# An output product in two slots and its sum in the third, weight sums at other places, a folded product loaded in place, and a gate behind a mask

## The chip, the cores and the metric

The kernel runs on one core of a Trainium2 chip, as one launch. The metric is the device time of that launch in microseconds. All arithmetic is in float32. Each float32 matrix product appears in the profile as two matmul records, and what the text calls one product is those two records.

## The reference

The input x is 8 sequences of 128 rows of 512 numbers. Two layers are computed, each of the form x = x + ffn(cond(x)).

- First layer. cond multiplies each sequence by one of 8 matrices of 512x512, chosen by an index. ffn is a 512x512 product with a bias, plus 8 experts of rank 16 of which the two with the largest gate values count, with softmax weights.
- Second layer, cond. Attention with 32 query heads and 8 key heads of 128 numbers: queries, keys and values are projected from x, queries and keys are normalised by their root mean square and rotated by their position, keys and values of 512 earlier positions come from 16 pages of a cache, positions beyond the sequence's length are masked, and after the softmax the outputs of all heads are multiplied by Wo (4096x512).
- Second layer, ffn. 64 experts of rank 8, of which the 16 with the largest scores count: `gate` is the softmax over the 16 largest of (x Wq_w^T) keys^T, and the output is ((x A_w^T) * gate) B_w^T * 2.

```python
probs = jax.nn.softmax(scores, axis=-1)
o = jnp.einsum('bhqk,bkhd->bqhd', probs, v_all)
...
gate = jnp.sum(jax.nn.one_hot(top_idx, NUM_EXPERTS, dtype=top_w.dtype) * top_w[..., None], axis=-2)
z_gated = (z * gate[..., None]).reshape(*z.shape[:-2], BOTTLENECK)
out = jnp.einsum('bsn,on->bso', z_gated, B_w) * SCALING
```

## The kernel before

**Units.** The attention is cut into 64 units, one for each of the 8 sequences and each of the 8 key heads, in the order: two key heads of a sequence, then the next sequence; after 16 units the next two key heads. A unit has four query heads, h = 0 to 3. `iteration(u)` writes the instructions of unit u, and with them, in the same four slots, work of other units: the output product of unit u-3, projections of units to come, and sums. The order of the instructions on each engine is written out by hand: what the program says first, an engine does first, and waits come only from the data. u runs from 1 to 66 (`NU` = 64). In the text r is u modulo 16.

**A slot (unit u, head h)** has: the two score products on TensorE (`scores`, L445 against the cached keys, L448 against the unit's own), into one of two PSUM buffers in turn; the mask and the row minimum on VectorE in one instruction (`mask_exp`, L458: the scores come negated, so "low" is what the exponential is shifted by); the exponential with its row sum on ScalarE (L469); for the head before it the reciprocal on VectorE (L474) and the multiplication on POOL (`normalize`, L475); from h = 2 on the transpose by 32x32 blocks on VectorE (`blocks`, L480, for head h-2). In slot 2 the queries of the unit after next are transposed as well (`blocks_qk`, L431), into the same buffer `pb`, of which there is one: it is free when the last unit's transfer out has read it. Then the output product and a part of the projections on TensorE (`project`, L268, with adds on VectorE, L271).

**The end of a unit**: `add_output(u-3, False)`, the copy of the next unit's queries and keys on ScalarE (`heads_qk`, L1019), weight loads on POOL's queue, `normalize` of head 3, `norms(u+3)` (squares on ScalarE, L317; then on POOL ss, L321, and rs, L323), `blocks` of heads 2 and 3, `exchange_out` (px, four DMAs, two on SP's and two on ScalarE's queue), `add_output(u-3, True)`, `rotate(u+3)` on VectorE (two L335 of 128x512, two L349, which need rs, then L352 and L353), and `values(u-2)` on TensorE (L1032). At the start of the next unit SP's queue holds page loads of keys, the query part of what was sent out (qkb), more page loads and the probabilities (pT), each behind the transfer out.

**The output product.** Four units (a pair of sequences, two key heads) and the parts of Wo for these two key heads, in two halves, are multiplied in the manner of Strassen and Winograd, with seven block products (`output`, L1157). v = u-3 is split into a pair p and a turn t = v modulo 4; turn 1 is u = 4, 8, 12, ..., 60. Up to p = 13 (u = 56) turn 1 has one product, A11 times B11, in four parts, one for each slot:

```python
elif t == 1 and p < WHOLE_PAIRS:
    product(0, (p, A11), B11, (h,))
```

Its result lies in the one PSUM buffer "y", which all turns use. `add_output(v, late)` adds it to the four quarters of the pair's output (`over(lo, 4)`: L1244 copies it for the first four pairs, L1226 adds it afterwards, 128x1024) as a late add, after `exchange_out`. Turn 2's first product writes the same buffer.

**Weight sums.** The projections use seven products as well, whose right sides are four parts of the weights (0 to 3, loaded by `load_q` at places listed in `LOADS_Q`) and four sums, T3, T2, T4 and T1 in the order in which they depend on each other (`sums_q`, L163, 128x768). Each group of 16 units needs new ones for two key heads: `sums_w` says in which slot and on which engine. Product 6 in slot 3 of r = 11 (and of r = 13 for the second key head) needs T2, product 7 at that unit's end needs T3, product 4 in slot 1 of the next unit needs T4, product 5 in its slot 2 needs T1.

**The ffn of the second layer** begins in the last units. Wq_w and keys are multiplied ahead (`l0_fold`) and kept in DRAM as `fold_d`, 128 x 4 x 64. `f_weights`, from unit 57 on, loads it and A_w and B_w into a tile `fw`; its part "sa" has, for each of four chunks, 64 columns "s" (the folded product) and 512 columns "a" (A_w). `fold_d` is first loaded into a part of its own, "f", and copied to "s" on VectorE (`f_fold`, L856) in slot 1 of unit 59. At the end of unit 59 `f_first_products(0)` multiplies the first sequence's rows (fq and fr, L987), copies two halves away on ScalarE, adds the scores and at once makes the gate's weights (`f_weights_of`, L891 to L908: two times the eight largest, an exponential on ScalarE, sum and reciprocal). Before fq, slot 2 of unit 59 has the transposes of those rows and their copy on ScalarE (L866).

## Time and profile before

| | |
|---|---|
| median of 3 runs | 1203.69 us (1202.99 to 1205.12) |
| the profiled execution | 1204.42 us, span 1202.7 us |
| TensorE | 1187.0 us busy (99%) |
| VectorE | 937.2 us (78%) |
| POOL (GpSimd) | 773.3 us (64%) |
| ScalarE | 507.1 us (42%) |
| L1157, the output products | 206.6 us busy, 784 records |
| L163, weight sums on POOL | 26 of 1.82 us |
| L163, weight sums on VectorE | 6, of 0.93 to 2.56 us |
| L856, the copy of the folded product | 1 of 2.82 us |

The profile is of one execution; PE is TensorE's matmuls, PEld its weight loads, DVE is VectorE, ACT ScalarE, POOL GpSimd, SP SyncE, which here issues transfers. A line of a timeline has the start and the length in microseconds, the engine, the line of the kernel, the operation, the tiles written and read, the shape and the count, and in brackets how long the engine had been idle and what ended that. A line of the waits has who waited for whom, the sum in microseconds, how often, and the longest. Ends of matmuls are modelled; the distance from one start to the next is measured.

### The profile page before, as it was taken

The numbers are of one execution on the slowest core, as the hardware profiler recorded it, in microseconds if no ns is written. First come the engines' busy times: TensorE is split into PE (matmuls) and PEld (weight loads), VectorE is DVE, ScalarE is ACT, GpSimd is POOL, SyncE is SP. The second block draws the span as 40 slices with busy tenths as digits, with TensorE's granted clock in tenths as the row PEclk, the third lists the DMA queues.
The fourth block names the chain that finished last, engine by engine and source line by source line (L and its number), as shares of the span: only waits on it lengthen the run. The fifth ranks groups of instructions, "written<-read, shape, count | busy, mean of one in ns | idle before, by whom it ended". The sixth has DMA issues, their size and how long they took to land.

```text
span 1202.7 us, 17039 instructions
## 1 busy us (share of the span) xinstructions
PE 1187.0 (99%) x4196; PEld 721.1 (60%) x4196; DVE 937.2 (78%) x2141; ACT 507.1 (42%) x1469; POOL 773.3 (64%) x867
## 2 busy tenths in 40 slices
PE   9999999999999999999999999999999999999998
PEld 7666545565555556555556565555655555655567
DVE  2557788777888787878888887878888888887757
ACT  1345534443444444444444444444444444444321
POOL 3544869778755687678756685677656684665432
PEclk9999999999999999999999999999999999999999
DMA  8823777888878988889789988887889878888653
GB/s 316 311 70 119 249 239 242 262 271 261 265 254 253 310 246 269 262 294 286 247 254 293 282 246 273 283 272 243 268 257 310 271 249 250 266 288 265 193 156 113
DMA packets 205447, 302.35 MB, mean 251 GB/s; under 512 B 84771, under 2 KB 119332, under 8 KB 204324
## 3 DMA queue, kind: packets, MB, share of 16 engines
q1 hardware_dynamic: 170164, 196.29, 53.4%
q10 hardware_dynamic: 18864, 52.57, 13.2%
q0 software_dynamic: 16320, 52.40, 12.3%
q8 instruction: 34, 0.56, 0.2%
q14 instruction: 65, 0.53, 0.1%
HBM read 185.44 MB, written 115.74 MB: 250 GB/s over the span
## 4 chain that ended last, share of the span: by engine, by line
PE 84%; POOL 4%; DMA 4%; DVE 3%; issue 2%; ACT 1%; SPq 1%; ACTq 0%; DVEq 0%; POOLq 0%
PE o L1032 19%; PE p L268 18%; PE s L445 16%; PE y L1157 12%; PE s L448 4%; PE p L301 3%; DMA px<-pb 3%; PE cp L633 2%; PE bp L655 2%; PE y L1170 2%; POOL wqkv L163 1%; POOL p L475 1%; PE op L987 1%; DVE pb L480 1%; DVE xo L1662 1%
## 5 line engine op out<-in xcount | busy, mean ns | idle before, releaser
L469 ACT ACTIVATE p<-p,low 128x640 f32<-128x640 f32 x256 | 211.8, 828 | 442.7 <-DVE den L474 275.6
L475 POOL TENSOR_SCALAR p<-p,den 128x640 f32<-128x640 f32 x256 | 211.4, 826 | 219.9 <-DVE den L474 218.7
L268 PE MATMUL p<-wqkv,xo 128*128 128x384 f32 x784 | 281.3, 487 | 2.2 <-POOL wqkv L163 2.0
L458 DVE CUSTOM_DVE_ANT_0 p<-s,mask,rs 128x640 f32<-128x640 f32 x256 | 222.2, 878 | 68.9 <-PE s L448 68.1
L445 PE MATMUL s<-kt,qkT 128*128 128x512 f32 x504 | 258.0, 593 | 3.7 <-DVE low L458 3.6
L1032 PE MATMUL o<-pT,vt 128*128 128x512 f32 x512 | 230.3, 592 | 0.0
L480 DVE STREAM_TRANSPOSE pb<-p 128x640 f32<-128x640 f32 x248 | 204.8, 827 | 29.5 <-POOL p L475 29.4
L1157 PE MATMUL y<-wo,oT 128*128 128x256 f32 x784 | 206.6, 380 | 2.4 <-DVE yp L1226 1.6
L268 PEld LDWEIGHTS p<-wqkv,xo 128*128 128x128 f32 x784 | 148.1, 190 | 72.2 <-POOL wqkv L163 4.0
L448 PEld LDWEIGHTS s<-qkT 128*128 128x128 f32 x504 | 95.8, 190 | 120.5 <-issue 120.5
L209 POOL DMA_INDIRECT vt<-in_vc,vrow x128 | 138.7, 1083 | 41.4 <-issue 31.5
L1032 PEld LDWEIGHTS o<-pT,vt 128*128 128x128 f32 x512 | 97.0, 190 | 108.0 <-issue 92.8
L445 PEld LDWEIGHTS s<-kt,qkT 128*128 128x128 f32 x504 | 95.0, 190 | 74.3 <-issue 28.0
L1157 PEld LDWEIGHTS y<-wo,oT 128*128 128x128 f32 x784 | 131.8, 191 | 11.6 <-issue 1.8
L317 ACT ACTIVATE sq<-c 128x128 f32<-128x128 f32 x320 | 98.9, 309 | 9.5 <-DVE oT L480 1.4
L448 PE MATMUL s<-qkT 128*128 128x128 f32 x504 | 96.8, 274 | 0.0
L323 POOL TENSOR_TENSOR rs<-ss,mhalf 128x5 f32<-128x5 f32 x64 | 84.5, 1321 | 5.3
L1055 ACT COPY oT<-o 128x512 f32<-128x512 f32 x64 | 37.5, 585 | 103.3 <-PE o L1032 77.9
L431 DVE STREAM_TRANSPOSE pb<-ca 128x640 f32<-128x640 f32 x60 | 50.3, 838 | 29.1 <-DMA kt<-in_kc 16.6
L321 POOL TENSOR_SCALAR ss<-ss,eps 128x5 f32<-128x5 f32 x64 | 22.7, 355 | 72.2 <-ACT sq L317 72.2
L1032 PE MATMUL o<-pT,vn 128*128 128x512 f32 x128 | 65.4, 592 | 0.0
L271 DVE TENSOR_TENSOR c<-c,p 128x384 f32<-128x384 f32 x84 | 44.7, 532 | 21.4 <-PE p L268 21.4
(301 smaller groups left out, 1511.0 us busy)
## 6 DMA issues: line engine op xcount, KB each, us to landing
pT<-px SPq DMA_DIRECT2D x64, 1280.0 KB, 6.6
px<-pb SPq DMA_DIRECT2D x120, 400.0 KB, 5.5
px<-pb ACTq DMA_DIRECT2D x120, 400.0 KB, 5.7
qkb<-px SPq DMA_DIRECT2D x60, 320.0 KB, 4.3
kt<-in_kc SPq DMA_DIRECT2D x512, 32.0 KB, 5.4
wqkv<-in_wqkv POOLq DMA_DIRECT2D x32, 384.0 KB, 5.2
wo<-in_wo POOLq DMA_DIRECT2D x17, 512.0 KB, 8.2
yd<-yp POOLq DMA_DIRECT2D x12, 512.0 KB, 9.8
```

Of the source, the lines that this page charges most:

```text
L209: nc.gpsimd.indirect_dma_start(out=kv_t[step][1][:, c, :], out_offset=None, in_=vc, in_offset=bass.IndirectOffsetOnAxis(ap=vrow[:, hf, at ...
L268: nc.tensor.matmul(out=ps, lhsT=xo[:, pr, x, c, :], rhs=w[:, c, :], start=(c == 0), stop=(c == 1))
L317: nc.scalar.activation(sq, cs[:, at : at + D], AF.Square, accum_out=ss[:, h : h + 1])
L323: nc.gpsimd.tensor_tensor(rs, ss, mhalf, ALU.pow)
L445: nc.tensor.matmul(out=s[:, :L], lhsT=qkT[:, h, :], rhs=kt[:, :, g % GH, :], start=True, stop=True)
L448: nc.tensor.matmul(out=s[:, L:NK], lhsT=qkT[:, h, :], rhs=qkT[:, REP, :], start=True, stop=True)
L458: nc.vector.tensor_tensor_reduce(out=p, in0=s_t.pop((u, h))[:, :NK], in1=mask_t[st], scale=rs_t[u][:, h : h + 1], scalar=BIG, op0=ALU.add, ...
L469: nc.scalar.activation(p, p, AF.Exp, bias=low, scale=-1.0, accum_out=den)
L475: nc.gpsimd.tensor_scalar(p_t[u, h], p_t[u, h], den, 1.0, ALU.mult, ALU.mult)
L480: nc.vector.transpose(pb_t[u][:, :, h * w : (h + 1) * w].rearrange("p i (j a) -> p j i a", a=32), p_t.pop((u, h)).rearrange("p (j i a) -> ...
L1032: nc.tensor.matmul(out=o, lhsT=vt[:, c, j * D : (j + 1) * D] if c < LC else vn_t.pop(u), rhs=pT[:, c], start=(c == 0), stop=(c == LC),)
L1157: nc.tensor.matmul(out=y_t["y"][:, half * HN : (half + 1) * HN], lhsT=part(key)[:, i * S : (i + 1) * S], rhs=wo_t[:, slot(w, key[0] // (B ...
```

## The change

- In turn 1 up to p = 13, two of the four parts of the product are done in slot 0 and two in slot 1. Its add moves from the unit's end to slot 2, ahead of `new_pb` and `blocks_qk`. It is no longer late, and the call at the end of the unit leaves turn 1 out.
- For the first key head T3 moves from slot (11, 0) to (9, 2), and T2, T4 and T1 each take the slot of the one before; for the second, T3 moves from (12, 2) to (12, 1), T2 from (13, 1) to (12, 2), T1 from VectorE to POOL in the same slot (13, 1). T4 stays on VectorE.
- `fold_d` is loaded straight to "s"; the part "f" and `f_fold` go.
- The gate's weights of the first sequence are made in slot 1 of unit 60, behind that slot's mask; the scores are still added at the end of unit 59. For the other sequences nothing changes.

```diff
@@ -841,19 +841,15 @@
         if piece == 0:
             w = wp.tile([P, 7 * 2 * HW], F32, tag="wqkv", name="fw", bufs=GH)
             at = 0
-            for n, width in (("sa", E1 + DM), ("b", DM), ("f", E1)):
+            for n, width in (("sa", E1 + DM), ("b", DM)):
                 fw_t[n] = w[:, at : at + NC * width].rearrange("p (c n) -> p c n", c=NC)
                 at += NC * width
             fw_t["s"], fw_t["a"] = fw_t["sa"][:, :, :E1], fw_t["sa"][:, :, E1:]
-            nc.gpsimd.dma_start(out=fw_t["f"], in_=fold_d)
+            nc.gpsimd.dma_start(out=fw_t["s"], in_=fold_d)
         n, c = ("a", piece) if piece < 2 else ("b", piece - 3)
         if piece != 2:
             src = (aw if n == "a" else bw).rearrange("(c p) n -> p c n", p=P)
             nc.gpsimd.dma_start(out=fw_t[n][:, 2 * c : 2 * c + 2], in_=src[:, 2 * c : 2 * c + 2])
-
-    def f_fold():
-
-        nc.vector.tensor_copy(fw_t["s"], fw_t["f"])
 
     ORDER = (0, 1, 4, 2, 3, 5, 6, 7)
 
@@ -1138,17 +1134,18 @@
                 return
             r, g = u % 16, (u // 16 + 1) * GH
             do = {
-                (11, 0): (0, 3),
-                (11, 1): (0, 2),
-                (11, 2): (0, 4),
-                (12, 0): (0, 1),
-                (12, 2): (1, 3),
-                (13, 1): (1, 2),
+                (9, 2): (0, 3),
+                (11, 0): (0, 2),
+                (11, 1): (0, 4),
+                (11, 2): (0, 1),
+                (12, 1): (1, 3),
+                (12, 2): (1, 2),
+                (13, 1): (1, 1),
             }.get((r, h))
             if do is not None:
                 sums_q(nc.gpsimd, g + do[0], do[1])
-            if (r, h) in ((13, 1), (13, 3)):
-                sums_q(nc.vector, g + 1, {1: 1, 3: 4}[h])
+            if (r, h) == (13, 3):
+                sums_q(nc.vector, g + 1, 4)
 
 
         def product(half, key, w, chunks):
@@ -1186,8 +1183,8 @@
                     product(0, (p - 1, A12), B22, two)
                 else:
                     product(1, (p - 1, A21), T1, two)
-            elif t == 1 and p < WHOLE_PAIRS:
-                product(0, (p, A11), B11, (h,))
+            elif t == 1 and p < WHOLE_PAIRS and h < 2:
+                product(0, (p, A11), B11, two)
             elif t == 2:
                 if 0 < p <= WHOLE_PAIRS and h < 2:
                     product(1, (p - 1, A11), T2, two)
@@ -1239,7 +1236,7 @@
                     drop((p - 1, A21), (p - 1, A12))
                 else:
                     add(y[:, 1::2], over(hi, 2))
-            elif t == 1 and late:
+            elif t == 1 and not late:
                 if p < B // 2:
                     nc.vector.tensor_copy(yp_t[p], over(lo, 4))
                 else:
@@ -1363,7 +1360,13 @@
             nc.scalar.copy(m1, one[:, E1:])
             nc.scalar.copy(m2, two[:, E1:])
             sb = room(b)[0]
-            wf_t[b] = f_weights_of(f_scores([one[:, :E1], two[:, :E1]], sb), sb)
+            sc_t[b], sb_t[b] = f_scores([one[:, :E1], two[:, :E1]], sb), sb
+            if p:
+                f_first_weights(p)
+
+        def f_first_weights(p):
+            b = 2 * p
+            wf_t[b] = f_weights_of(sc_t.pop(b), sb_t.pop(b))
 
         def f_step(p, *which):
             if p not in steps_t:
@@ -1514,13 +1517,13 @@
                         load_o(u // 16, (1, B12))
 
                     if h == 2:
+                        if (u - 3) % 4 == 1 and 0 <= u - 3 < 4 * WHOLE_PAIRS:
+                            add_output(u - 3, False)
                         new_pb(u)
                         if u + 2 in range(4, NU):
                             blocks_qk(u + 2, u)
                     if h > 1:
                         blocks(u, h - 2)
-                    if h == 1 and u == NU - 5:
-                        f_fold()
                     if u == NU - 5 and h == 1:
                         t4 = wo_t[:, 6, : 2 * (E1 + HN)].rearrange("p (c n) -> p c n", c=2)
                         fw_t["qa"], qa_steps[:] = quarters_of(
@@ -1533,6 +1536,8 @@
                         fw_t["qa"][M1], fw_t["qa"][M2] = (sa[:, c : c + 2, : E1 + HN] for c in (0, 2))
                         fw_t["qa"][M4] = t4
                     at = (u - NU + 5, h)
+                    if at == (1, 1):
+                        f_first_weights(0)
                     if at == (1, 0):
                         nc.vector.tensor_copy(fw_t["qa"][M4][:, :, :E1], fw_t["s"][:, 2:])
                     if at in ((0, 1), (0, 2), (1, 0), (1, 1)):
@@ -1567,7 +1572,7 @@
 
                 if (u, h) in WHOLE:
                     project_whole(1, *WHOLE[u, h])
-            if on(u - 3):
+            if on(u - 3) and ((u - 3) % 4 != 1 or u - 3 >= 4 * WHOLE_PAIRS):
                 add_output(u - 3, False)
             if on(u + 1) and (u + 1) % GH == 0:
                 make_mask(units[u + 1][0])
```

## The prediction

> **What bounds the kernel now.** I read the page first, then the waits of TensorE, then the timeline around each of those waits.
>
> ```profile
> PE 1187.0 (99%) x4196; PEld 721.1 (60%) x4196; DVE 937.2 (78%) x2141; ACT 507.1 (42%) x1469; POOL 773.3 (64%) x867
> PEclk9999999999999999999999999999999999999999
> ```
>
> TensorE is busy for 99% of the span and its granted clock never drops, so nothing can be won except its idle time, and anything that makes it wait is added to the time. The change takes no matmul away. These are the waits of TensorE that touch what it edits:
>
> ```profile
> PE s L445 <- DVE low L458: 3.6, 2, 2.3
> PE p L268 <- POOL wqkv L163: 2.0, 2, 1.0
> PE y L1157 <- DVE yp L1226: 1.6, 1, 1.6
> ...
> PE fq L987 <- ACT rooms L866: 0.9, 1, 0.9
> PE y L1157 <- DVE yp L1244: 0.7, 1, 0.7
> ```
>
> Of the first line one wait (2.3 us, at 179 us) is in unit 5, the other (1.3 us, at 1077 us) in unit 60. Everything the change could remove is therefore 1.3 + 2.0 + 1.6 + 0.9 + 0.7 = 6.5 us. The view counts from modelled ends; from start to start of the matmuls the same waits are some 1.4 us larger together, 7.9 us.
>
> The waits that are not there yet matter as much. Below is VectorE (and one ScalarE-to-POOL link) in unit 32, which starts at 615.44 us and is a unit of the kind that the change re-orders (its output turn is 1), and at the start of unit 33:
>
> ```profile
> 621.04 0.88 DVE L458 CUSTOM_DVE_ANT_0 p<-s,mask,rs 128x640 f32<-128x640 f32 x1 [0.53 <-PE s L448]
> 621.92 0.82 DVE L431 STREAM_TRANSPOSE pb<-ca 128x640 f32<-128x640 f32 x1
> 624.30 0.87 DVE L458 CUSTOM_DVE_ANT_0 p<-s,mask,rs 128x640 f32<-128x640 f32 x1
> 627.43 0.84 DVE L480 STREAM_TRANSPOSE pb<-p 128x640 f32<-128x640 f32 x1 [0.18 <-POOL p L475]
> 628.20 1.18 DVE L1226 TENSOR_TENSOR yp<-yp,y 128x1024 f32<-128x1024 f32 x1
> 629.31 0.68 DVE L335 TENSOR_TENSOR ca<-c,tab 128x512 f32<-128x512 f32 x1
> 631.08 0.35 DVE L349 SCALAR_TENSOR_TENSOR ca<-c,rs,tab 128x128 f32<-128x128 f32 x1 [0.49 <-POOL rs L323]
> 632.53 0.88 DVE L458 CUSTOM_DVE_ANT_0 p<-s,mask,rs 128x640 f32<-128x640 f32 x1
> ```
> ```profile
> 628.96 0.27 POOL L321 TENSOR_SCALAR ss<-ss,eps 128x5 f32<-128x5 f32 x1 [1.56 <-ACT sq L317]
> 629.31 1.73 POOL L323 TENSOR_TENSOR rs<-ss,mhalf 128x5 f32<-128x5 f32 x1
> ```
> ```profile
> 634.84 1.02 PE L445 MATMUL s<-kt,qkT 128*128 128x512 f32 x2
> ```
>
> The mask of head 2 waits for TensorE (0.53 us). From there a closed chain runs to the next unit's first mask: mask of head 3, exp, head copy and squares on ScalarE, ss and rs on POOL, L349, mask of head 0. That mask ends at 633.42, and the third score of unit 33, which needs its bank, starts at 634.84. So 1.42 us of slack stand between this chain and TensorE.
>
> **The product in two slots, the add in the third.** A 128x256 product is two records of 0.216 us from start to start. In a turn-1 unit heads 0 and 1 now carry four each and heads 2 and 3 none. TensorE's unit stays 14.21 us, but the score of head 2 starts 2 x 0.43 = 0.86 us later, and with it the mask. Behind that mask the add, one instruction and no DMA, now stands ahead of L431: 1.11 us from 628.20 to 629.31. L431 goes from 621.92 to 623.89, the mask of head 3 from 624.30 to 626.27, ss from 628.96 to 630.93, the last transpose from 627.43 to 629.40, all by 1.97 us. The add is gone behind that transpose, so the L335 pair starts at 630.17 and ends 1.27 us later at 631.44. ss then starts inside the pair. Where it does so in this profile it took much longer than 0.27 us, and ended when the pair had ended:
>
> ```profile
> 385.40 1.13 POOL L321 TENSOR_SCALAR ss<-ss,eps 128x5 f32<-128x5 f32 x1 [1.85 <-ACT sq L317]
> 386.61 1.20 POOL L323 TENSOR_TENSOR rs<-ss,mhalf 128x5 f32<-128x5 f32 x1
> ```
>
> There the pair began at 385.19. In unit 32 ss then ends near 631.59 (0.15 us behind the pair, as the one at 418.59 us did), rs runs 631.67 to 632.87, L349 starts at 632.90 and not 631.08. The mask ends 1.82 us later, at 635.24: 0.40 us past the slot of the score. A late score costs 0.06 us more to start, and its second record 0.10 us (as at 1077 us): 0.55 us of new wait. If ss met no pair, the chain would move by about 1.4 us and cost nothing to 0.15; with ss held until the pair ends as above it is 0.55. I take 0.55, since ss falls into the middle of the pair. Units 16, 20, 32, 36, 48, 52 and 56 are alike: 7 x 0.55 = 3.85 us lost, bound 0 to 1 below and 4 above.
>
> The Trainium skill, "SBUF — State Buffer", section "Who interferes with whom", says that a VectorE instruction with two SBUF inputs and a POOL instruction that reads SBUF exclude each other, the loser blocking wholly, and puts the release about 0.115 us behind the VectorE instruction. The row agrees; by the page's figure each of the seven would cost 0.03 us less.
>
> Units 8, 24, 40 have two weight loads issued on POOL between the last normalisations, so the L335 pair comes later: rs and pair start within 0.02 us of each other. Where the pair began with rs, rs took 1.73 (as above), otherwise 1.20. Lost per unit: 0.7 or 0.2; I take 0.7, since in unit 32 as it is now the two also start together: 2.1 us. In unit 17 the exchange out of unit 16, 1.97 us late, delays L431 (it already waits 1.12 us there for it) and the heads' copy on ScalarE (0.97 us): about 0.6 us at unit 18, whose slack is 0.94. Elsewhere that lateness on the SP and ACT queues (px, then qkb, three page loads, pT) is hidden by 1.9 to 2.6 us of slack. The last page loads are issued 5.5 us or more ahead of the scores that need them. That cover shrinks by 1.4 us; gone, it would cost about 1 us each at units 18, 34 and 50.
>
> Gained: the waits for the late add (L1226, L1244: 0.92 us in unit 13, 0.37 in 29, 1.82 in 45, with their second records) go, but the chain is right behind them. In units 12, 28 and 44 the add fills a wait of L431 for px (1.5, 0.9, 2.3 us) and the chain up to ss moves by 0 to 0.3 us; rs stays where ScalarE's squares put it. What is left is 0.3, 0.4 and 0.6 us for the three groups of units 11-13, 27-29 and 43-45. This already contains the next part. Unit 5 gains 0.15, unit 41 its 0.27 us of small waits.
>
> **The sums sooner.** T3 goes from unit 11 to unit 9 (1.81 us on POOL, into the 2.43 us that POOL idles at 767 us; its two loads were issued 10 us before and landed in 5). T2 then takes T3's place, two slots ahead of the product that waited 1.0 us for it at 543 and 804 us. POOL still runs three sums in units 11, 27 and 43, is busy from 792 to 814 us with hardly a break, so the mask of unit 44 does not come sooner: most of the 2.3 us turns into a wait for that mask. In units 12 and 13 POOL has as many sums as before, and one that took 2.5 us leaves VectorE, where it cost TensorE nothing (the mask behind it had 8.6 us of slack).
>
> **Fold in place, first gate later.** L856 took 2.82 us on VectorE in unit 59, and held up the exp, the copy L866 and so fq (1.15 us from start to start). The gate's weights, 13 small instructions from 1073.11 to 1076.06, stood before the mask of unit 60 for which the third score waited 1.52 us. Both waits go: 2.67 us. But the weights now stand between the masks of heads 1 and 2 (their exp on ScalarE behind the exps of heads 0 and 1, which are done by then), and the copy of unit 59 is followed by L431, which px (landed near 1061.7) holds anyway. So VectorE ends unit 60 only 1.1 us sooner, while TensorE is 2.67 sooner, and the slack of 0.90 us at unit 61 is overdrawn by about 0.8. Gain 1.85 us, between 1.0 and 2.67. The load in place has four pieces of 256 bytes for each partition in place of one of 1 KB; it landed in 5.8 us and has 25 us.
>
> The skill's "DMA: Bandwidth & Descriptors", section "Specifications", speaks against it: under 512 B a transfer loses line rate. No run here shows the price for this load; at four times 5.8 us it would still be covered.
>
> If the two weight loads of unit 57 have to wait on POOL for the fold, whose pieces lie between theirs, POOL stands for up to 5.8 us, and unit 58 (slack 2.6) loses about 2.5 us. Nothing in this trace shows such a wait or excludes it; I take nothing.
>
> **The sum.** Gains 0.3 + 0.4 + 0.6 + 0.15 + 0.27 + 1.85 = 3.6 us; losses 3.85 + 2.1 + 0.6 = 6.55 us; net 2.95 us slower. The profiled execution took 1204.42 us (span 1202.7 and 1.7 around it), 0.7 above the median of 1203.69. On that median: 1206.6 us.
>
> **The rivals.** (1) The chain has room: ss does not meet the pair, or TensorE's reorder shifts the mask by less than 0.86. It decides at a shift of 1.36 us; below it the seven and the three cost nothing, and 3 to 4 us are gained: 1200 us. For it: the forecast overdraws by only 0.4 us; against it: the rows on ss. (2) Same mechanism, half its size (0.25 us for each unit, 0.2 for 8, 24 and 40): losses 2.9, a net of 0 to +2, no difference that a measurement here can tell from none (0.2%, 2.4 us, is that bound). (3) The fold or the page loads wait too: 2.5 to 4 us more, 1209 to 1210.
>
> **How the numbers follow.** Forecast 0.43, (1) 0.20, (2) 0.27, (3) 0.10. Faster 0.20, same 0.27, slower 0.53. The range leaves out half of (1) and the far end of (3): 1200.0 to 1210.0.
>
> **What would show it.** Right: in turn-1 units L431 about 2 us later in the unit, ss about 0.9 us long, and short waits of TensorE for "low" at the third score of units 17, 21, 33, 37, 49, 53, 57; no wait for L163 or L1226; no L856; fq without a wait; a wait of under 1 us at unit 61. Wrong: no such waits for "low", or POOL standing at the weight loads of unit 57.

## The result, and the profile after

The changed kernel is slower: a median of 1212.97 us (1210.36 to 1218.93, 6 runs) against 1203.34 us (1199.54 to 1205.12, 6 runs) of the kernel before beside it, a ratio of 1.0087 with a 95% interval of 1.0058 to 1.0115. The forecast was 1206.6 us, between 1200.0 and 1210.0. Slower was right; the forecast loss of 2.9 us was less than a third of the measured one. The profiled execution of the changed kernel took 1210.36 us (span 1208.6), 5.9 us more than the one of before.

Two lines of its page, engines and granted clock:

```profile
PE 1191.0 (99%) x4196; PEld 721.2 (60%) x4196; DVE 930.4 (77%) x2137; ACT 505.2 (42%) x1469; POOL 775.5 (64%) x870
PEclk9999999999999999999999999999999999999999
```

The matmuls are the same 4196 and the clock is as before. What is new stands in TensorE's waits (after the change L1223, L1154, L1028 are what L1226, L1157, L1032 were):

```profile
PE s L445 <- DVE low L458: 9.1, 16, 2.0
PE p L268 <- DVE c L271: 2.3, 4, 0.7
...
PE y L1154 <- DVE yp L1223: 0.7, 1, 0.7
```

The waits for the weight sums (L163) and for fq are gone. In their place a score waits 16 times, and no longer twice, for "low", and there is a line that the forecast did not have: the projection's product L268 waits four times for the add L271 of an earlier projection. The forecast left no wait for the add of the output product either; one of 0.7 us is new in unit 44, those of units 13 and 45 are gone.

The first kind is the forecast's chain. Unit 32 of the changed kernel (TensorE starts unit 33 at 631.99), timeline of VectorE, POOL and TensorE:

```profile
624.23 0.88 DVE L458 CUSTOM_DVE_ANT_0 p<-s,mask,rs 128x640 f32<-128x640 f32 x1 [0.53 <-PE s L448]
625.12 1.20 DVE L1223 TENSOR_TENSOR yp<-yp,y 128x1024 f32<-128x1024 f32 x1
626.23 0.84 DVE L431 STREAM_TRANSPOSE pb<-ca 128x640 f32<-128x640 f32 x1
628.63 0.87 DVE L458 CUSTOM_DVE_ANT_0 p<-s,mask,rs 128x640 f32<-128x640 f32 x1
632.53 0.65 DVE L335 TENSOR_TENSOR ca<-c,tab 128x512 f32<-128x512 f32 x1
633.10 0.68 DVE L335 TENSOR_TENSOR sa<-c,tab 128x512 f32<-128x512 f32 x1
635.23 0.35 DVE L349 SCALAR_TENSOR_TENSOR ca<-c,rs,tab 128x128 f32<-128x128 f32 x1 [1.45 <-POOL rs L323]
636.69 0.88 DVE L458 CUSTOM_DVE_ANT_0 p<-s,mask,rs 128x640 f32<-128x640 f32 x1
```
```profile
633.28 0.64 POOL L321 TENSOR_SCALAR ss<-ss,eps 128x5 f32<-128x5 f32 x1 [1.56 <-ACT sq L317]
634.00 1.19 POOL L323 TENSOR_TENSOR rs<-ss,mhalf 128x5 f32<-128x5 f32 x1
```
```profile
637.63 1.13 PE L445 MATMUL s<-kt,qkT 128*128 128x512 f32 x2 [0.30 <-DVE low L458]
```

Every link is where the forecast put it: the mask of head 2 later by two products, the add ahead of L431, the mask of head 3 behind it, ss inside the L335 pair (0.64 us and not 0.27, ended 0.14 us behind the pair), rs until 635.19, L349, the mask, and then the third score, which is late.

Unit by unit (from the first score of a unit to that of the next), against the first profile of before; the changed kernel was profiled twice (the second is the first experiment below):

| units | forecast, us | changed kernel | once more |
|---|---|---|---|
| 21, 37, 53, 57 | +2.20 | +2.29 | +2.32 |
| 17, 33, 49 | +1.65 | **+4.51** | **+4.24** |
| 9, 25, 41 | +1.83 | +2.07 | +2.08 |
| 18, 19 | +0.6 | +0.27 | +1.06 |
| 11 to 13, 27 to 29, 43 to 45 | -1.3 | -2.05 | -2.28 |
| 5 | -0.15 | -0.30 | -0.30 |
| 59 to 61 (fold and gate) | -1.85 | **-0.90** | **-0.27** |
| sum | +2.98 | +5.89 | +6.85 |

(In the forecast's sum unit 41 stands as 0.7 lost and 0.27 gained, and the parts are rounded to 2.95.)

### The profile page after: what moved, and what is told of

It is laid out like the page before. It is cut to its first block, busy times and chain, and to the rows that moved or that the text cites. A ratio compares the mean times of both kernels' runs of the same rounds, so it can differ in the third digit from the quotient of the medians.

```text
span 1208.6 us, 17029 instructions
## 1 busy us (share of the span) xinstructions
PE 1191.0 (99%) x4196; PEld 721.2 (60%) x4196; DVE 930.4 (77%) x2137; ACT 505.2 (42%) x1469; POOL 775.5 (64%) x870
## 4 chain that ended last, share of the span: by engine, by line
PE 62%; DVE 10%; DMA 9%; POOL 8%; issue 5%; ACT 4%; SPq 1%; ACTq 1%; DVEq 0%; POOLq 0%
PE o L1028 13%; PE p L268 12%; PE s L445 11%; PE y L1154 9%; DMA px<-pb 7%; PE s L448 3%; DVE pb L480 3%; PE p L301 3%; POOL p L475 2%; PE cp L633 2%; PE bp L655 2%; ACT sq L317 2%; PE y L1167 2%; DVE p L458 1%; POOL rs L323 1%
## 5 line engine op out<-in xcount | busy, mean ns | idle before, releaser
L475 POOL TENSOR_SCALAR p<-p,den 128x640 f32<-128x640 f32 x256 | 207.3, 811 | 220.4 <-DVE den L474 219.3
L268 PE MATMUL p<-wqkv,xo 128*128 128x384 f32 x784 | 281.7, 487 | 2.3 <-DVE c L271 2.3
L1028 PE MATMUL o<-pT,vt 128*128 128x512 f32 x512 | 230.3, 592 | 0.0
L480 DVE STREAM_TRANSPOSE pb<-p 128x640 f32<-128x640 f32 x248 | 204.7, 826 | 27.7 <-POOL p L475 27.6
L1154 PE MATMUL y<-wo,oT 128*128 128x256 f32 x784 | 201.9, 380 | 0.8 <-DVE yp L1223 0.7
L268 PEld LDWEIGHTS p<-wqkv,xo 128*128 128x128 f32 x784 | 146.1, 190 | 70.4 <-DVE c L271 5.2
L209 POOL DMA_INDIRECT vt<-in_vc,vrow x128 | 136.5, 1066 | 40.1 <-issue 30.6
L1028 PEld LDWEIGHTS o<-pT,vt 128*128 128x128 f32 x512 | 97.0, 190 | 108.0 <-issue 92.8
L1154 PEld LDWEIGHTS y<-wo,oT 128*128 128x128 f32 x784 | 134.0, 191 | 11.2 <-PE s L448 1.1
L431 DVE STREAM_TRANSPOSE pb<-ca 128x640 f32<-128x640 f32 x60 | 50.5, 841 | 49.5 <-DMA kt<-in_kc 23.0
L321 POOL TENSOR_SCALAR ss<-ss,eps 128x5 f32<-128x5 f32 x64 | 28.1, 440 | 76.7 <-ACT sq L317 76.6
L1028 PE MATMUL o<-pT,vn 128*128 128x512 f32 x128 | 65.4, 592 | 0.0
L1223 DVE TENSOR_TENSOR yp<-yp,y 128x512 f32<-128x512 f32 (+3 forms) x94 | 60.1, 640 | 0.0
```

Source lines behind the costliest of these rows:

```text
L209: nc.gpsimd.indirect_dma_start(out=kv_t[step][1][:, c, :], out_offset=None, in_=vc, in_offset=bass.IndirectOffsetOnAxis(ap=vrow[:, hf, at ...
L268: nc.tensor.matmul(out=ps, lhsT=xo[:, pr, x, c, :], rhs=w[:, c, :], start=(c == 0), stop=(c == 1))
L475: nc.gpsimd.tensor_scalar(p_t[u, h], p_t[u, h], den, 1.0, ALU.mult, ALU.mult)
L480: nc.vector.transpose(pb_t[u][:, :, h * w : (h + 1) * w].rearrange("p i (j a) -> p j i a", a=32), p_t.pop((u, h)).rearrange("p (j i a) -> ...
L1028: nc.tensor.matmul(out=o, lhsT=vt[:, c, j * D : (j + 1) * D] if c < LC else vn_t.pop(u), rhs=pT[:, c], start=(c == 0), stop=(c == LC),)
L1154: nc.tensor.matmul(out=y_t["y"][:, half * HN : (half + 1) * HN], lhsT=part(key)[:, i * S : (i + 1) * S], rhs=wo_t[:, slot(w, key[0] // (B ...
```

## The experiments

"Profile" below is the sum over the units from unit 4 on against the first profile of before (for the changed kernel, over the rows of the table above); "ratio" is that of the times to the kernel before on the same chip, with its 95% interval.

**Both kernels once more.** No edit.

> The changed kernel once more. Its profiled execution was 5.9 us longer than the one of before (1210.36 against 1204.42), its median over six executions 9.6 us longer. If the trace tells the whole loss, the profile lies 5 to 7 us above the profile of before again, and the median near 1210 us. If there is a loss that the one profile does not show, the median comes out near 1213 again and some of the executions near 1210.

> The kernel before, once more, for a second profile of it. The medians of before and changed kernel differ by some 10 us, the two profiles by 5.9 and 6.9. If the first profile of before was one of its longer executions, this one is shorter (near 1201 us), and shows at which unit an execution of the same kernel differs from another; if it is 1204 again, the profiles leave something out.

The changed kernel: profile +6.85 us, 1213.20 us, ratio 1.0091 (1.0064 to 1.0118). The kernel before against itself: profile -1.51 us, 1200.04 us, ratio 0.9985 (0.9970 to 0.9999), which is what a ratio near 1 is worth here. Its second profile differs from the first around the sums: unit 27 is 1.27 us shorter (the wait for T2 that the forecast counted at 543 us is gone without any edit), unit 13 0.81 longer, unit 5 0.71 and unit 29 0.43 shorter; the units of turn 2 that the change made longer agree to 0.00, but for unit 41 (-0.13). So the losses are of the kernel, and a part of the gains is of the execution. The gap between times and profiles stays open in part. The two profiled executions of before (1204.42, 1203.26) are above its medians, those of the changed kernel (1210.36, 1211.84) below its own: 7.3 us apart on the mean, where the medians are some 11 apart. The granted clock is not the difference: over the executions whose mean clock is 1.00 the medians are 1200.9 us (48 of the kernel before) and 1212.05 us (8 of the changed one), 11 apart as well. What the other 4 us are no profile shows.

**The product alone, and the rest alone.** The first is the kernel before with only this:

```diff
-            elif t == 1 and p < WHOLE_PAIRS:
-                product(0, (p, A11), B11, (h,))
+            elif t == 1 and p < WHOLE_PAIRS and h < 2:
+                product(0, (p, A11), B11, two)
...
+                        if (u - 3) % 4 == 1 and 0 <= u - 3 < 4 * WHOLE_PAIRS:
+                            add_output(u - 3, False)
                         new_pb(u)
```

The second is the changed kernel with this undone.

> The kernel before, with the product of turn 1 in two slots and its add in the third, nothing else. Theory (the chain mask of head 2, add, L431, mask of head 3, ss, rs, mask of the next unit is pushed 1.97 us): all the losses of the changed kernel are here, +0.6 us for each of units 21, 37, 53, 57, +0.7 for 9, 25, 41, +1.5 for 17, 33, 49, together about 9 us, less 1 to 2 us at units 12 to 14, 28 to 30 and 44 to 46: 7 to 8 us slower than before, so slower than the changed kernel. Rival (the other parts cost the time: more sums on POOL, the gate's weights between masks): this kernel lies within 2 us of before.

> The changed kernel with the product of turn 1 in four slots and its add late, as before; sums sooner, fold in place and first gate later stay. Theory: 1 to 2 us faster than before (fold and gate 0.9 us net as in units 59 to 61 of the changed kernel; of the two waits for T2, 2 x 1.26 us, most turns into a wait for the masks of units 28 and 44). Rival (the other parts cost the time): slower than before by 3 us or more.

Product alone: profile +15.95 us, ratio 1.0139 (1.0102 to 1.0176), twice what was expected. The rest alone: -0.70 us, ratio 1.0001 (0.9979 to 1.0022), a little less than expected. So the product's place costs the time, and the parts do not add: 15.95 - 0.70 is not 5.89. The ten units of turn 2 lose the same, within 0.15 us, with or without the sums moved. The difference is in the units of the sums, 13, 27, 29, 43 and 45 (7.6 us together), in unit 5 (2.5 us; the clock, last section) and in unit 60, which is 2.05 us longer (unit 61 is 1.77 shorter). In the product alone TensorE waits 4.8 us in five places for L163, before 2.0 us in two. In unit 43 its three sums on POOL start 1.56 us later against TensorE, as ss of the unit before does (1.46 us into the unit, before 0.11 ahead of it). Read off the units, the sums moved sooner win that back: the three groups of units from 11 to 13, 27 to 29 and 43 to 45 are 6.4 us shorter with them. That is argued and not isolated: no run has the product and the sums without fold and gate, and single units of these groups differ by up to 1.3 us between executions.

**The add late again, the product still in two slots.**

```diff
-                        if (u - 3) % 4 == 1 and 0 <= u - 3 < 4 * WHOLE_PAIRS:
-                            add_output(u - 3, False)
...
-            elif t == 1 and not late:
+            elif t == 1 and late:
```

> The changed kernel with the add at the unit's end again, the product still in two slots. The mask of head 2 is then 0.86 us late and nothing stands in front of L431. Theory (the add in front of L431 makes the 0.86 to 1.97, and the pair L335 then meets ss): the chain moves by 0.9 us where 1.42 are free, the waits at units 17, 21, 33, 37, 49, 53, 57 go (0 to 0.2 us each), the waits for the late add at 13, 29 and 45 come back: between 2 us faster and 1 us slower than before. Rival (the product in two slots is itself the cause: head 2's score late): 4 us or more slower than before.

Profile -0.54 us, ratio 1.0019 (0.9996 to 1.0041). Units 17, 33, 49, 21, 37, 53, 57 are back to 0.01 or better; units 9, 25, 41 keep 0.79, 0.78 and 0.67. So the two products' shift of 0.86 us fits into the slack of the seven, and it is the add ahead of L431 that overdraws it, as the theory has it. For 9, 25, 41 the 0.86 alone is enough.

**The pair L335 ahead of the last transpose**, in units of turn 1 from 4 to 56 (`sooner`).

```diff
                 blocks(u, REP - 2)
+                if sooner(u):
+                    rotate_q(u + 3)
                 blocks(u, REP - 1)
...
-                rotate(u + 3)
+                if not sooner(u):
+                    rotate_q(u + 3)
+                rotate_k(u + 3)
```

> The changed kernel, with the two L335 in units of turn 1 ahead of the last transpose, so that they are over when ss and rs start. Theory (part of the lateness is that ss, and in units 8, 24 and 40 rs, run against that pair): ss of these units takes 0.27 us and no longer 0.64 to 0.9, rs 1.2; the mask of the next unit comes 0.3 to 0.5 us sooner, and units 21, 37, 53, 57 fall from 0.57 over before to 0.1 to 0.3, units 9, 25, 41 from 0.72 to 0.2 to 0.4. The transfer out is about 1 us later, which can cost something in units 17, 33 and 49. Rival (the shift by the add alone makes the wait): ss shortens but units 21, 37, 53, 57 stay at 0.5 or more.

Profile +2.15 us, ratio 1.0059 (1.0038 to 1.0080). POOL and VectorE at the end of unit 36, first the changed kernel (TensorE starts unit 37 at 698.11), then this one (at 695.05):

```profile
699.40 0.64 POOL L321 TENSOR_SCALAR ss<-ss,eps 128x5 f32<-128x5 f32 x1 [1.56 <-ACT sq L317]
700.12 1.19 POOL L323 TENSOR_TENSOR rs<-ss,mhalf 128x5 f32<-128x5 f32 x1
701.35 0.35 DVE L349 SCALAR_TENSOR_TENSOR ca<-c,rs,tab 128x128 f32<-128x128 f32 x1 [1.45 <-POOL rs L323]
```
```profile
696.35 0.27 POOL L321 TENSOR_SCALAR ss<-ss,eps 128x5 f32<-128x5 f32 x1 [1.56 <-ACT sq L317]
696.70 1.19 POOL L323 TENSOR_TENSOR rs<-ss,mhalf 128x5 f32<-128x5 f32 x1
697.93 0.35 DVE L349 SCALAR_TENSOR_TENSOR ca<-c,rs,tab 128x128 f32<-128x128 f32 x1 [1.24 <-POOL rs L323]
```

ss starts at the same place in the unit (1.29 and 1.30 us behind TensorE's start), takes 0.27 and not 0.64, and L349 comes 0.36 us sooner (2.88 behind the start and not 3.24). The wait of units 21, 37, 53, 57 falls by as much, from 0.57 to 0.20 to 0.34. So the pair's 0.36 us is about two thirds of that wait, and the shift the rest. In units 9, 25 and 41 it won nothing (0.77, 0.76, 0.64): there the pair met the multiplication of head 3 on POOL instead, which took 1.54 us and not 0.82 in unit 8. Units 17, 33 and 49 fell from 1.5 to 0.25 to 0.29, which was not expected; the transfer out of unit 16, sent 0.85 us later in the unit, landed 1.2 us sooner. Why, no run here shows.

**The projection's add ahead of L431 in units 17, 33 and 49.** The second wait by itself. In unit 17 of the changed kernel:

```profile
380.29 0.85 DVE L431 STREAM_TRANSPOSE pb<-ca 128x640 f32<-128x640 f32 x1 [2.94 <-DMA kt<-in_kc]
381.06 0.80 DVE L480 STREAM_TRANSPOSE pb<-p 128x640 f32<-128x640 f32 x1
381.79 0.52 DVE L271 TENSOR_TENSOR c<-u,p 128x384 f32<-128x384 f32 x1
```
```profile
382.36 1.56 PE L268 MATMUL p<-wqkv,xo 128*128 128x384 f32 x4 [0.62 <-DVE c L271]
```

L431 waits 2.94 us for the transfer out of unit 16 (the profile names a page load; the query part qkb, which needs that same transfer, is issued at 380.25 as well, and in units 33 and 49, where L431 waits 2.98 and 3.01 us, the profile names the transfer). The add L271 stands behind L431 and L480 on VectorE, and TensorE needs its bank. The kernel before, unit 17:

```profile
377.73 0.85 DVE L431 STREAM_TRANSPOSE pb<-ca 128x640 f32<-128x640 f32 x1 [1.12 <-DMA kt<-in_kc]
379.22 0.52 DVE L271 TENSOR_TENSOR c<-u,p 128x384 f32<-128x384 f32 x1
```

There the add ended 1.09 us ahead of the product that needs its bank (380.83). The edit (`behind`: u modulo 16 is 1):

```diff
                     if h == 2:
-                        new_pb(u)
-                        if u + 2 in range(4, NU):
-                            blocks_qk(u + 2, u)
+                        if not behind(u):
+                            new_pb(u)
+                            blocks_qk_of(u)
...
                     project(k, j, slots[h - 1 : h])
+                if h == 2 and behind(u):
+                    new_pb(u)
+                    blocks_qk_of(u)
+                    blocks(u, 0)
```

> The changed kernel, but in units 17, 33 and 49 L431 and the first transpose of slot 2 stand behind the projection of that slot and its add, and no longer ahead of them. Theory (in these three, L431 waits 2.9 us for the transfer out of the unit before, the projection's add stands behind it on VectorE, and TensorE waits for the bank of that add): the waits of L268 for c go, units 17, 33, 49 fall from 1.5 us over before to about 0.6 as in units 21, 37, 53: 2.3 to 2.8 us faster than the changed kernel in the profile. Rival (these units lose more because the same chain of ss is later there, the mask or page loads): no change of more than 0.3 us a unit.

The three units fell to 0.59, 0.57 and 0.58, the size of the other four, and no L268 waits for c in them: the theory holds for them. In the sum nothing was won: profile +7.99 us, ratio 1.0093 (1.0059 to 1.0127). Units 18, 19, 34 and 35 took it back (+0.85, +1.31, +0.20, +1.18), which fits L431 being as late as it was while TensorE arrives sooner.

**The rotation behind a mask of the next unit.** If L349 no longer stands ahead of the first mask, the chain ends without TensorE (`later`: units of turn 1).

```diff
             if u + 3 < NU:
-                rotate(u + 3)
+                if not later(u):
+                    rotate(u + 3)
...
+                    if h == 1 and later(u - 1) and u + 2 < NU:
+                        rotate(u + 2)
```

> The changed kernel, but what rotates the queries and keys of unit u+3 (the two L335, the two L349, L352, L353) is done, in units of output turn 1, behind the mask of head 1 of the next unit and no longer ahead of its mask of head 0. Theory (the masks of the next unit are late because L349 waits for rs, which the late chain of ss brings): units 21, 37, 53 and 57 go from 0.57 us over before to 0.0, units 9, 25 and 41 from 0.7 to 0.0, unit 61 from 1.8 to under 0.5, and units 17, 33 and 49 keep only the part that the projection's bank brings, 0.7 to 0.9 of their 1.5 us each: 6 to 8 us faster than the changed kernel, that is within 2 us of before. Rival (the masks are late because VectorE has more to do ahead of them, whatever waits for rs): the six instructions come back in the next unit, and at most half of that is won.

> Both edits of the two runs above in the changed kernel. If the two causes are separate and are all that the product's place costs, units 9, 17, 21, 25, 33, 37, 41, 49, 53 and 57 are all back at the length of before, and what is left is the gain of the other parts: 1 to 5 us faster than before. If they share a cause, it is no better than the better of the two.

The first: profile +46.52 us, ratio 1.0370 (1.0337 to 1.0403); with the edit for 17, 33, 49 as well: +36.29, ratio 1.0375 (1.0330 to 1.0419). Neither theory nor rival has such a number. In the first the waits for "low" are all but gone (0.8 us in two places); in the second units 17, 33, 49 are at 0.07, 0.00 and 0.00, but units 18, 19, 35 and 51 are 4.3 us longer, so the late transfer is still paid for. Whether the two causes are separate these runs cannot tell, as a new loss covers them: in the first TensorE waits 35.7 us for L271, and seven stretches of lower clock, 34 us together, go with these waits (last section). VectorE in unit 21, and POOL beside it:

```profile
452.69 6.35 DVE L349 SCALAR_TENSOR_TENSOR ca<-c,rs,tab 128x128 f32<-128x128 f32 x1
458.96 0.34 DVE L349 SCALAR_TENSOR_TENSOR sa<-c,rs,tab 128x128 f32<-128x128 f32 x1
```
```profile
453.02 0.74 POOL L242 TENSOR_TENSOR tab<-nw,cos 128x256 f32<-128x256 f32 x1
453.70 0.73 POOL L242 TENSOR_TENSOR tab<-nw,sin 128x256 f32<-128x256 f32 x1
454.39 1.26 POOL L1103 TENSOR_TENSOR wo<-wo 128x512 f32<-128x512 f32 x1
455.61 1.25 POOL L1212 TENSOR_TENSOR oT<-oT 128x512 f32<-128x512 f32 x1
456.86 0.80 POOL L475 TENSOR_SCALAR p<-p,den 128x640 f32<-128x640 f32 x1
457.63 1.25 POOL L1103 TENSOR_TENSOR wo<-wo 128x512 f32<-128x512 f32 x1
```

An instruction of 0.35 us took 6.35, until POOL's unbroken run of six instructions was over (458.88). From 150 us on, L349 was held like this ten times, for 2.67 to 6.38 us.

So the rotation was put behind the mask of head 0, where POOL has no such run (`if h == 0 and later(u - 1)`).

> The changed kernel, with the rotation of unit u+3 in units of turn 1 put behind the mask of head 0 of the next unit, where POOL has only ss, rs and two transfers to issue, and not behind the mask of head 1, where its multiplications and sums stand. Theory (the product's place costs time through L349, which waits for rs ahead of the mask; and the slower kernel with the rotation behind the second mask lost only because L349 there met a run of POOL's work): no instruction L349 over 1 us; units 21, 37, 53, 57 back at the length of before, units 9, 25, 41 too, units 17, 33, 49 at 0.7 to 0.9 over it; 4 to 8 us faster than the changed kernel, within 3 us of before. Rival (rotating behind a mask costs time wherever it stands, as VectorE is then late for the later heads): 5 us or more slower than before.

Profile +5.41 us, ratio 1.0066 (1.0050 to 1.0083): half a us better than the changed kernel, so the expected 4 to 8 us did not come, and the rival is right on the size. From 150 us on no L349 took over 0.41 us. Units 9, 25, 41 fell to 0.23, 0.25, 0.42, units 21, 37, 53, 57 only to 0.46, 0.16, 0.32, 0.43. The rotation's 2.7 us now stand ahead of L271, for which TensorE waits 6.7 us in nine places: 3.75 in units 17, 33 and 49, 1.7 in unit 5, and 0.1 to 0.3 in each of five others. Units 17, 33, 49 stayed at 1.52, and unit 17 shows why, VectorE and TensorE:

```profile
379.84 0.84 DVE L431 STREAM_TRANSPOSE pb<-ca 128x640 f32<-128x640 f32 x1 [3.57 <-DMA px<-pb]
```
```profile
381.90 1.56 PE L268 MATMUL p<-wqkv,xo 128*128 128x384 f32 x4 [1.25 <-DVE c L271]
```

With the wait for "low" gone TensorE comes sooner and waits as much longer for the bank: in these units the landing of the transfer sets the length, and the chain of ss lies under it.

**Fold alone, gate alone** (each is the part of the change's diff, in the kernel before).

> The kernel before with the folded product loaded in place and no other edit. By the prediction's step the wait for fq goes (unit 59: 1.15 us shorter) and what is behind L431 stays: 0.5 to 1.2 us faster in units 59 to 61 together. Rival: the gate's weights, still ahead of the first mask of unit 60, then cost more there (unit 60 longer by up to 1 us).

> The kernel before with the gate's weights in slot 1 of unit 60 and no other edit. By the prediction's step unit 60 is 1.52 us shorter and unit 61 up to 0.8 longer: 0.7 us faster or better. Rival (the chain of unit 60 is what counts, and the 13 instructions in it are as late there): unit 61 is longer by as much as unit 60 is shorter, nothing won.

| unit | fold alone | gate alone | both (changed kernel) |
|---|---|---|---|
| 59 | -1.15 | -1.15 | -1.15 |
| 60 | +3.31 | -1.52 | -1.52 |
| 61 | 0.00 | +2.65 | +1.77 |

Fold alone has a profile of -0.99 us, ratio 0.9997 (0.9978 to 1.0015); gate alone -2.70 us, ratio 0.9989 (0.9968 to 1.0010), with much of it in units 13, 27, 43 and 45, which differ between executions. Neither part wins anything by itself. The gate alone does what its rival says: unit 61 gives back what units 59 and 60 won. The fold alone lost three times what its rival allowed in unit 60, and the gate's weights are not all of that: in unit 59 of this profile L431 waited 2.95 us for a transfer and started 9.09 us into the unit, before at 7.72, and a part is the clock (last section). The -1.15 with the gate alone is a surprise, as the copy L856 is still there. Its line in the kernel before, and in the kernel with the gate alone:

```profile
1058.29 2.82 DVE L856 COPY fw<-fw 128x256 f32<-128x256 f32 x1
```
```profile
1055.90 0.48 DVE L856 COPY fw<-fw 128x256 f32<-128x256 f32 x1
```

In the kernel before the copy started 0.10 us behind POOL's second L242 and ended 0.16 us behind L948, the last of POOL's run (1060.94). With the gate alone it started 0.24 us ahead of the second L242 and got in between. The second profile of before has 2.75 us, the product alone 0.77.

**Versions that might beat both.** The product in two slots and the add in the third only in units 12, 28, 44, where L431 waits for its transfer anyway (`if u in (12, 28, 44)`); the same with the gate in slot 1 of unit 61; and all that helped together.

> The changed kernel with the product in two slots and the add in the third only in units 12, 28 and 44, where L431 waits longer for its transfer than the add takes; in every other unit of turn 1 the product is in four slots and the add late, as before. Theory (the add costs where it stands in front of an L431 that could have started): the losses at 9, 17, 21, 25, 33, 37, 41, 49, 53, 57 go, the gains at units 5, 13, 27, 29, 43, 45, 59 and 60 stay: 2.5 to 5 us faster than before. Rival (three units alone gain nothing): within 1.5 us of before, like the kernel with the rest alone.

> The kernel with the product in two slots in units 12, 28 and 44 only, and the first sequence's gate one unit later, in slot 1 of unit 61. Theory (the gate's 13 instructions in slot 1 of unit 60 push the same chain of mask, ss, rs and the next mask; unit 61 has no unit behind it whose rotation waits): unit 61 falls from 1.3 over before to under 0.4, units 59 and 60 keep their 2.67: about 1 us faster than the kernel with the three units, 2.5 to 4.5 us faster than before in the profile. Rival: the wait goes to unit 62 with the same size.

> The edits that the runs so far point to, together: product in two slots and add in the third in every unit of turn 1 but 16, 32, 48 (and 60); the rotation of these units behind the first mask of the next; sums sooner; fold in place; gate in slot 1 of unit 61. If the theory holds at every place: no waits left for low, none for the late add but in 17, 33, 49 none at all: 4 to 6 us faster than before. If the rotation behind the mask costs something: slower than the kernel with three units.

Three units: profile -1.72 us, ratio 0.9996 (0.9977 to 1.0014). All ten units but 53 (+0.52) are back at 0.00 or better, and units 27, 43, 59 and 60 keep -1.27, -1.25, -1.15 and -1.52; unit 61 (+1.31) and units 44 and 52 (+0.87, +0.83) take some of it back. Gate in 61: profile +1.06, ratio 1.0003 (0.9993 to 1.0014): unit 61 fell to 0.89, not to under 0.4, and unit 62 rose by 0.66, which is the rival; its unit 5 is 2.35 us longer (last section). Why unit 61 keeps 0.89 us is on ScalarE: VectorE ends unit 60's last transpose 1.7 us sooner than in the kernel with the three units, but the copy of the heads, ahead of the squares that ss needs, now waits for the query part of what was sent out:

```profile
1084.07 0.72 ACT L1015 COPY qkT<-qkb 128x640 f32<-128x640 f32 x1 [1.56 <-DMA qkb<-px]
```

ss starts 16.17 us into unit 60, in the kernel with the three units at 16.22. All together: profile +1.17, ratio 1.0015 (1.0005 to 1.0025), and not the 4 to 6 us faster that were expected. None is faster than the kernel before by what can be measured.

## Why the forecast fell short

**The chain.** Right, in every link and in size: 0.55 us forecast for each of seven units, 0.56 to 0.59 measured in the four where nothing else is at work. The two runs on it separate its terms: the two products' 0.86 us alone cost these units nothing (add late), and the pair is 0.36 of the 0.57 (pair sooner). Without the pair the forecast had nothing to 0.15 us left; 0.20 to 0.34 were. Its list of signs has ss at 0.9 us; its own sum makes 0.66 (630.93 to 631.59), and 0.64 was measured. The Trainium skill's "SBUF — State Buffer", section "Who interferes with whom", drawn on for it, agrees on ss: an instruction on POOL that meets the pair waits for its end. The 0.115 us that the prediction gives with it stands elsewhere on that page, for the descriptors of a transfer behind a VectorE copy; here ss ended 0.14 us behind the pair.

**Units 9, 25, 41.** Right: 0.62 to 0.74 each for 0.7 less unit 41's small waits.

**The step that failed** is the one on unit 17: "In unit 17 the exchange out of unit 16, 1.97 us late, delays L431 ... about 0.6 us at unit 18". The late transfer and the waiting L431 were seen. Behind L431 on VectorE's queue I counted only ScalarE's copy, and not the projection's add L271, whose bank TensorE needs in the same unit; and I did it for unit 17 alone and not for 33 and 49, where L431 waits 1.01 and 1.22 us before and 2.98 and 3.01 after: for them "Elsewhere that lateness ... is hidden" put the late transfer at nothing. The term was 0.55 for each of the three units; they lost 1.25 to 1.56. That is 2.6 to 2.9 us, nearly all of the difference between the forecast's 2.95 us and the first profile's 5.9. Nor is the bank all of it: with the add put first, units 18, 19, 34 and 35 were 3.5 us longer than before, so what was priced too low is the late transfer, wherever TensorE meets it. Rival (3), 2.5 to 4 us more and 1209 to 1210 us, had the size of the profiles' difference, by luck, as its cause was not there: POOL issued the fold and the next weight load back to back (1040.83 and 1041.66 us), and no wait of TensorE is put down to a page load. The medians' difference of 9.6 us no rival had. Rival (2) is wrong in its sum: losses of 2.9 against gains of 3.6 make 0.7 us faster and not "0 to +2".

**Fold and gate.** Mis-sized: 1.85 us forecast, 0.90 and 0.27 measured. The two waits went (2.67 us, as forecast), but unit 61 gave back 1.77 and 2.40 and not 0.8 (its wait is 1.3 and 2.0 us, where the list of signs had under 1). The gate's 13 instructions in slot 1 push the masks of heads 2 and 3 of unit 60 and so the same chain, and a copy ahead of them (L1542, 128x128) takes 1.27 us, before 0.22 (L1537). From the start of unit 59 the first mask of unit 61 comes 0.35 us sooner, where the forecast had VectorE end unit 60 1.1 us sooner. Behind the gate the transfer waits at nearly the same place, as the kernel with the gate in unit 61 shows. And the price of L856 that the step began from, 2.82 us, was a price of POOL's work beside it. Its load in pieces of 256 bytes landed in 6.2 us, against 5.8 before. The fourfold was the prediction's own bound; the Trainium skill's "DMA: Bandwidth & Descriptors", section "Specifications", states only that a transfer needs 512 bytes for line rate; this load landed 0.4 us later.

**The gains at the sums.** More than forecast (2.05 and 2.28 us for 1.3), of which 1.27 at unit 27 came in the kernel before too when it was profiled again.

**The median.** The sum was set on 1203.69 us. Of the 94 executions of the kernel before that the experiments brought the median is 1202.0, and 82 are under the 1204.42 of the profiled one that the sum was made against.

## What to carry to other kernels

Where an instruction is put ahead of one that waits for a transfer, list everything behind it on that queue and who needs it, unit by unit, and ask of each unit which of two waits ends last: taking one away here showed the other at the same size. The price of a VectorE instruction in a profile holds only for what POOL was doing beside it; before one is moved, or counted as a saving, look at POOL's row in both places. Gains of about 1 us at waits that one profile shows want a second profile of the same kernel.

## What was not expected of the hardware

**A held instruction can stay held for a whole run.** The 6.35 us above: POOL's instructions follow one another without a gap, and VectorE's got its turn only when POOL stopped. In each of the ten cases L349 ended 0.14 to 0.16 us behind an instruction of POOL's that was followed by a gap; 0.07 us was enough once. It is not always so: in units 13 and 29 an L349 of 2.12 us ended 0.24 us behind one of POOL's instructions while the run went on. The section of the Trainium skill named above has the exclusion, and says that who issues first decides it. The rows neither show nor refute the second part. L349 started 0.33 us ahead of the first of the six and lost, but POOL was then at L209, an indirect transfer (451.82 to 453.00), and in unit 17 of the same kernel an L349 that started under an L209 took 0.93 us and ended 0.27 us behind it.

**A wait of TensorE of 2.3 us or more can be followed by a lower granted clock.** The kernel with the gate alone has a wait for "low" in unit 5 of 2.89 us, and the windows after it show TensorE's clock (the number behind POOL's busy time):

```profile
180.27 2.08 PE L445 MATMUL s<-kt,qkT 128*128 128x512 f32 x2 [2.89 <-DVE low L458]
```
```profile
180.00:182.00 2.00, 1.73 (x2) 0.84 (x3) 1.18 (x5) 1.69 (x5) 1.98 (x4) 0.50 0.99 326
182.00:184.00 2.00, 2.00 (x8) 1.60 (x7) 1.07 (x4) 0.61 (x3) 2.00 (x2) 0.72 0.73 215
184.00:187.00 3.00, 3.00 (x13) 1.98 (x12) 2.58 (x4) 0.72 (x2) 3.00 (x4) 1.00 0.53 131
```

The kernel before waits 2.33 us there and its clock stays at 1.00. Unit 5 is 2.06 us longer with the gate alone, of which 0.56 is the wait. From unit 3 on, over all the profiles, no wait of up to 2.22 us went with this, and each of the eleven of 3.2 us or more did (in the two kernels with the rotation behind the second mask). In between the length does not decide: 2.28 us (all together, in unit 5), 2.73 (product alone), 2.75 (unit 60 of the fold alone, a part of its +3.31), 2.84, 2.89 and 2.90 (gate in 61) went with it; 2.33 (before), 2.36, 2.50 (three units), 2.74, 2.79 and 2.83 did not. Each time the clock was at 0.50 for 3.41 us or for 6.83, twice that, and in the kernel with the rotation behind the second mask the seven stretches begin whole multiples of 3.41 us apart. That would fit a clock that is judged over fixed stretches of 3.41 us, of which a wait fills more or less; no run tests it. A wait of 2.3 us or more can so cost more than itself, and the kernel before is not clear of it: 46 of its 94 executions in the experiments have a mean clock of 0.997 to 0.999, and one stretch of 3.41 us at half clock makes 0.999 by estimate. The Trainium skill, "TensorE: Matmul & The Clock Gate", Part 1, has the halved clock, after an idle window of about 3.4 us; the rows agree on the half (0.50) and on the 3.41 us, and show it after waits of 2.3 to 2.9.
